# Adaptive layer norm with a Mamba block: the input of seven half sequences loaded with its channels on the partitions

## The chip, the core and the metric

The kernel runs on one core of a Trainium2 chip. The metric is the device time of one execution in microseconds (us); three executions of the kernel before gave 735.45, 736.16 and 738.33 us, so its median is 736.16 us. A profiled execution took 737.38 us, of which the profile's span covers 735.7 us.

## The reference

The input `x` has 4 sequences of 512 tokens with 512 channels. For each sequence a small matrix product of `silu(c)` with `wmod` gives six vectors over the channels: shift, scale and gate for each of two branches. The first branch is a Mamba2 mixer, the second a linear layer with binarized weights:

```
h = layernorm(x) * (1 + ca) + sa            # over the 512 channels of a token
xBCzA = h @ in_proj_w.T                     # 2048 + 1024 + 64 columns
xBC = silu(causal depthwise conv of 4 taps over the tokens)
dt = softplus(A_log); chunked scan over chunks of 128 tokens, 64 heads
x = x + ga * ((y + D * x_in) * silu(z)) @ out_proj_w.T
x = x + gb * (layernorm(x) * (1 + cb) + sb) @ (sign(w) * mean|w|).T + ...
```

The convolution and the projections want the normed input with its channels on the partitions (the contraction runs over partitions); the statistics of a token are sums over its channels. This is the place of the change.

## The kernel before

The 2048 tokens are cut into eight half sequences of T = 256 tokens (index `h`, two for each sequence, `HPB` = 2). Each half has a front (norm, projections, convolution, steps towards the scan), eight units of the scan (two chunks `c` of 128 tokens times four pairs of head groups `gp`) and a tail for each chunk (output projection, second norm, second linear layer, store).

**The order of the work.** A list of steps, one for each unit, is written out by hand at the end (L787 to L863). While the units of half `h` - 1 run as steps (h-1)*8 to (h-1)*8+7, the front of half `h` is interleaved: FRONT puts `load_x` at relative step 1, `f_norm` at 2, `f_hT` and `f_dt` at 3, then the projections `f_B`, `f_C`, `f_x`, `f_z` to step 10. For half 1 the list SECOND has `load_x` at 0, `f_norm` at 1, `f_hT` and `f_dt` at 2; half 0 has FIRST and runs ahead of all units. In one step the order written is: fronts and tails (within a step, entries of half 0 such as `load_wout` and `signs` come before those of half 1), `burst`, `stage2` of this step's unit, then `stage0` and `stage1` of the unit two steps later. The framework that builds the program lays each engine's instructions in a fixed queue; it prefers this written order, but draws an instruction ahead when its inputs and its buffer are free by its own reckoning. On the chip each queue then runs strictly in that order: an instruction that waits holds up all behind it on its engine, DMA issues on SP and POOL too.

**The lines that matter here.** `load_x` (L75) brings a half as two tiles of 128 tokens by 512 channels, tag `xa`, three buffers, on SP's queue (L79). `f_norm` (L307) calls `layer_norm` (L289): DVE's statistics (L295, L296), epsilon (L297), POOL's power of -1/2 (L298, tile `rs_a`) and DVE's in-place subtract and multiply with a value for each partition (L300). `f_hT` (L335) has TensorE turn the tiles, eight transposes of 128x128 into two PSUM tiles `phT` (L330), and ACT write `hT` from them with the modulation as scale and bias, four activations of 128x256 (L347). `hT` (tag `hT`, two buffers) holds the three last tokens of the half before in its first columns (L340, L342). `f_dt` (L353) starts with TensorE's product `pa` (L368) and goes over some twenty small DVE and ACT operations to three stores in DRAM (`sums_d`, `e_d`, `r_d`), which POOL issues for all halves but the first (L389, L393, L407). Later these come back by SP as broadcast loads: `decay` (L541, L542), `e` (L582) and `rr` (L502, tag `rr`, two buffers, read by POOL at L507). ACT makes exponentials of `decay` (L549), DVE multiplies them (L625), TensorE uses them (`py`, L212 and L215).

**Around the first halves** SP's queue also carries the late weights: `wout` (2 MB, L265, once the modulation products `pg` no longer need its place), and the four tiles `fw` of the second layer's weights (L272), which take the places of `sg` and `ab`, tiles of the gates that `late_mods` works out on DVE (L256 to L260) and stores by SP (L262).

```
for step, f, args in (FIRST, SECOND)[h] if h < 2 else FRONT:
    at(max(0, h - 1) * NU + step, f, h, *args)
...
at(2, load_wout)
for o in range(NK):
    at(o // 2 + 2, signs, o)
```

Of the kernel before, what the change touches and what calls it, by code (L numbers as in the profile page):

```python
# [11 lines left out]
F32 = mybir.dt.float32  # L12
AF = mybir.ActivationFunctionType
# [3 lines left out]
P = 128  # L17

B, L, DM = 4, 512, 512
# [3 lines left out]
KS = 4  # L23
# [3 lines left out]
T = 256  # L27
NHALF = B * L // T
HPB = L // T
NK = DM // P  # L30
# [10 lines left out]
def adaln_mamba_block(  # L41
    ctx: ExitStack,
    tc: tile.TileContext,
    x: bass.AP,
    w_inT: bass.AP,
    conv_w: bass.AP,
    conv_b: bass.AP,
# [9 lines left out]
    nc = tc.nc  # L57
# [6 lines left out]
    def bc_mid(ap, n):  # L64

        return ap.unsqueeze(1).to_broadcast([ap.shape[0], n, ap.shape[1]])

    keep = ctx.enter_context(tc.tile_pool(name="keep", bufs=1))
    dram = ctx.enter_context(tc.tile_pool(name="dram", bufs=1, space=bass.MemoryType.DRAM))
    ps = ctx.enter_context(tc.tile_pool(name="ps", bufs=5, space=PSUM))  # L70
    wk = ctx.enter_context(tc.tile_pool(name="wk", bufs=2))

    xs_of = {}

    def load_x(h, queue=nc.sync):  # L75
        tiles = []
        for j in range(2):
            xt = wk.tile([P, DM], F32, tag="xa", name=f"x_{h}_{j}", bufs=3)
            queue.dma_start(xt, x[h * T + j * CH : h * T + (j + 1) * CH, :])  # L79
            tiles.append(xt)  # L80
        xs_of[h] = tiles


    ct = keep.tile([P, NK, B], F32, name="ct")
    nc.sync.dma_start(ct, cT)
    load_x(0, nc.scalar)


# [29 lines left out]
    modT = keep.tile([P, 4, NK, B], F32, name="modT")  # L118
    gate_d = dram.tile([B, 3, DM], F32, name="gate_d")
    sums_d = dram.tile([NHALF, 2, NH, CH], F32, name="sums_d")  # L120
    e_d = dram.tile([NHALF, 2, NH, CH], F32, name="e_d")
    r_d = dram.tile([NHALF, NH, 2, CH], F32, name="r_d")

# [80 lines left out]
    def scale_small():  # L204

        for v in (cw, cb, zb):
            nc.vector.tensor_scalar(v, v, 0.5, None, ALU.mult)
# [9 lines left out]
    def first_row(t6, copy):  # L217

        pg = ps.tile([P, DM], F32, tag="mm", name=f"pg{t6}")
        for k in range(NK):  # L220
            mm(pg[32 * k : 32 * k + 32, :], sc[:, k, :], wms[t6, k], start=True, stop=True)
        row = wk.tile([P, DM], F32, tag="h2", name=f"row{t6}")
        copy(row, pg)
        return row

    def first_turn(t6, slot, row):

        pm = ps.tile([P, NK, B], F32, tag="mm", name=f"pm{t6}")
        for dt in range(NK):
            mm(pm[:, dt, :], row[:, dt * P : (dt + 1) * P], sel, start=True, stop=True)  # L230
        nc.vector.tensor_scalar(modT[:, slot], pm, 1.0 if t6 == 1 else 0.0, None, ALU.add)
# [54 lines left out]
        nc.scalar.activation(bwT[:, :, o * P : (o + 1) * P], pt, AF.Copy, scale=2.0 / DM)  # L286


    def layer_norm(tiles, name, into=None):  # L289
        n = len(tiles)  # L290
        st = wk.tile([P, n, 6], F32, tag=f"st{n}", name=f"st_{name}")
        mv = wk.tile([P, n, 2], F32, tag=f"mv{n}", name=f"mv_{name}")
        rs = wk.tile([P, n], F32, tag=f"rs{n}", name=f"rs_{name}")
        for j, t in enumerate(tiles):
            nc.vector.bn_stats(st[:, j, :], t)  # L295
            nc.vector.bn_aggr(mv[:, j, :], st[:, j, :])  # L296
        nc.vector.tensor_scalar(rs, mv[:, :, 1], EPS, None, ALU.add)  # L297
        nc.gpsimd.tensor_tensor(rs, rs, mhalf[:, :n], ALU.pow)  # L298
        for j, t in enumerate(tiles):
            nc.vector.tensor_scalar(  # L300
                into[j], t, mv[:, j, 0:1], rs[:, j : j + 1], ALU.subtract, ALU.mult
            )


    H = [dict(B={}, C={}, xt={}, xs={}, bt={}, z={}) for _ in range(NHALF)]

    def f_norm(h):  # L307
        H[h]["xn"] = xs_of.pop(h)
        layer_norm(H[h]["xn"], f"a{h}", H[h]["xn"])

    def f_first(h):

        f_norm(h)
        for xp in xpads:
            nc.gpsimd.memset(xp, 0.0)
        for et in decays:
            nc.gpsimd.memset(et[CH // 2 :, :, 0 : CH // 2], 0.0)
        rows = first_row(1, nc.vector.tensor_copy), first_row(0, nc.scalar.copy)
        turned = [turned_x(h, d2) for d2 in range(NK // 2)]
        first_turn(1, 1, rows[0])  # L320
        first_turn(0, 0, rows[1])
        f_hT(h, turned)
        scale_small()

    def turned_x(h, d2):
        pt = ps.tile([P, 2, T], F32, tag="mm", name=f"phT_{h}_{d2}")
        for q in range(2):
            dt = 2 * d2 + q
            for j in range(2):
                nc.tensor.transpose(  # L330
                    pt[:, q, j * CH : (j + 1) * CH], H[h]["xn"][j][:, dt * P : (dt + 1) * P], ident
                )
        return pt

    def f_hT(h, turned=None):  # L335
        b = h // HPB

        hT = wk.tile([P, NK, KS - 1 + T], F32, tag="hT", name=f"hT_{h}")
        if h % HPB == 0:
            nc.gpsimd.memset(hT[:, :, 0 : KS - 1], 0.0)  # L340
        else:
            nc.gpsimd.tensor_copy(hT[:, :, 0 : KS - 1], H[h - 1]["hT"][:, :, T:])  # L342
        for d2 in range(NK // 2):
            pt = turned[d2] if turned else turned_x(h, d2)
            for q in range(2):
                dt = 2 * d2 + q
                nc.scalar.activation(  # L347
                    hT[:, dt, KS - 1 :], pt[:, q, :], AF.Identity,
                    bias=modT[:, 0, dt, b : b + 1], scale=modT[:, 1, dt, b : b + 1],
                )  # L350
        H[h]["hT"] = hT

    def f_dt(h):  # L353

# [2 lines left out]

        hT = H[h]["hT"]

# [369 lines left out]
    def tail1(h, c):  # L729
        b = h // HPB  # L730
        x2 = tails[h, c]
        po = ps.tile([P, DM], F32, tag="mm", name=f"po_{h}_{c}")
        last = (h, c) == (NHALF - 1, 1)
        for g in range(NKI):
            if last and g == NKI - 2:

                with tc.issue_after(last_po.ins):
                    tail2(h, 0)
            last_po = mm(po, H[h]["z"][g // 2][:, g % 2, c * CH : (c + 1) * CH], wout[:, g, :],  # L739
                         start=(g == 0), stop=(g == NKI - 1))  # L740
        t = wk.tile([P, DM], F32, tag="t", name=f"t_{h}_{c}", bufs=1)
        nc.vector.tensor_mul(t, po, gates[b][:, 0, :])
        nc.vector.tensor_add(x2, x2, t)
        layer_norm([x2], f"f{h}_{c}", [t])
        nc.gpsimd.tensor_add(x2, x2, gates[b][:, 2, :])
        tails[h, c] = (x2, t)
        if last:
            with tc.issue_after(last_po.ins):
                tail3(h, 0)
# [31 lines left out]
    def behind(h, f, *args):  # L781
# [4 lines left out]

    FRONT = [  # L787
        (1, load_x, ()), (2, f_norm, ()), (3, f_hT, ()), (3, f_dt, ()),
        (4, f_B, (0,)), (4, f_C, (0,)), (5, f_x, (0,)), (5, f_x, (1,)),
        (6, f_B, (1,)), (6, behind, (f_turned_sums,)), (6, f_C, (1,)), (6, behind, (f_xt, 0)),  # L790
# [4 lines left out]

    FIRST = [
        (-1, f_first, ()), (-1, first_dt, ()), (-1, f_B, (0,)), (-1, f_C, (0,)), (-1, f_x, (0,)),
        (-1, f_turned_sums, ()), (-1, f_Bt, (0,)), (-1, f_x, (1,)), (-1, behind, (f_xt, 0)),
        (-1, f_z, (0,)), (-1, behind, (f_xt, 1)),
# [4 lines left out]

    SECOND = [
        (0, load_x, ()), (1, f_norm, ()), (2, f_hT, ()), (2, f_dt, ()), (2, f_B, (0,)), (3, f_C, (0,)), (3, f_x, (0,)),
        (4, f_x, (1,)), (4, behind, (f_turned_sums,)),
        (5, f_B, (1,)),
# [31 lines left out]
    h = NHALF - 1  # L840
# [65 lines left out]
```

## Time and profile before

| | |
|---|---|
| median of three executions | 736.16 us (735.45 to 738.33) |
| profiled execution, its span | 737.38 us, 735.7 us |
| granted TensorE clock, mean | 0.993 |
| TensorE (PE) busy | 700.4 us, 95% |
| VectorE (DVE) busy | 599.5 us, 81% |
| ScalarE (ACT) busy | 522.0 us, 71% |
| GpSimd (POOL) busy | 254.8 us, 35% |
| moved by DMA | 99.24 MB, 135 GB/s in the mean |
| transposes `phT` (L330), all eight halves | 64, 273 ns median each as recorded |
| activations into `hT` (L347) | 32, 564 ns median |
| norm of `x` on DVE (L300) | 16, 546 ns median |

Busy time counts an instruction from its start to its modelled end; matmuls overlap one another, so eight of them take less time than eight times one. A stretch of the span is judged by its own rows: which engine has no gaps there, and what ended the gaps of the others. A line such as "PE pa <- ACT hT" names an instruction that sat idle and the one whose end released it.

### The profile page before, as it was taken

Reading aid. Unit: us, or ns where it says so; the run is one execution under the profiler, and the core shown is the slowest. Engines: PE = TensorE matmul, PEld = TensorE weight load, DVE = VectorE, ACT = ScalarE, POOL = GpSimd, SP = SyncE. Lnnn points to the kernel's source line nnn. Section 1 sums busy time; section 2 is a strip of 40 time slices with the busy share of each in tenths; the row PEclk is TensorE's granted clock in tenths of the full one; section 3 lists DMA queues with packets and bytes.
Section 4 is the critical chain, followed back from the end, with each engine's and each line's share of the span. In section 5 each row is a group of like instructions: output and inputs, shape, how many; then the busy total and the mean of one; then the engine's idle time right before and its main releaser. Section 6 shows DMA issues by size and latency. Waiting matters only on the chain.

```text
span 735.7 us, 15007 instructions
## 1 busy us (share of the span) xinstructions
PE 700.4 (95%) x5196; PEld 500.8 (68%) x5196; DVE 599.5 (81%) x1170; ACT 522.0 (71%) x1507; POOL 254.8 (35%) x297
## 2 busy tenths in 40 slices
PE   6999979899999999999999999999999999999997
PEld 3786746666677666677677666776667866677754
DVE  3869888876998678986899768996799867996995
ACT  2467658748696697785976787865968768788941
POOL 4021323444243332343223342433414332333652
PEclk9999989999999999999999999999999999999999
DMA  8991693535555256444644256552564537457720
GB/s 279 328 291 41 204 208 85 135 98 142 127 132 144 63 155 137 102 115 102 159 116 130 53 116 168 142 137 53 140 132 114 130 86 176 116 150 151 142 69 29
DMA packets 119067, 99.24 MB, mean 135 GB/s; under 512 B 73984, under 2 KB 97152, under 8 KB 118992
## 3 DMA queue, kind: packets, MB, share of 16 engines
q1 hardware_dynamic: 117808, 96.39, 52.3%
q0 software_dynamic: 896, 1.38, 0.7%
q8 instruction: 41, 0.67, 0.4%
q10 hardware_dynamic: 288, 0.52, 0.2%
q14 instruction: 34, 0.28, 0.1%
HBM read 92.47 MB, written 5.79 MB: 134 GB/s over the span
## 4 chain that ended last, share of the span: by engine, by line
PE 65%; ACT 16%; DVE 9%; DMA 4%; issue 4%; POOL 1%; SPq 1%; ACTq 0%; DVEq 0%; POOLq 0%
PE po L739 14%; PE pp_x L434 11%; PE pp_z L434 10%; ACT decay L549 9%; PE pp_C L434 7%; PE pp_B L434 5%; PE pf L775 3%; PE py L212 2%; PE py L215 2%; DVE decay L625 2%; ACT h L759 2%; DVE u_x L454 2%; DMA fw<-in_ffn_w 2%; ACT win L549 2%; PE gy L215 2%
## 5 line engine op out<-in xcount | busy, mean ns | idle before, releaser
L549 ACT ACTIVATE decay<-decay,st 128x128 f32<-128x128 f32 x960 | 293.9, 395 | 4.2 <-DMA decay<-sums_d 3.7
L625 DVE SCALAR_TENSOR_TENSOR decay<-decay,gm 128x1024 f32<-128x1024 f32 x120 | 160.8, 1341 | 50.3 <-ACT decay L549 47.2
L434 PE MATMUL pp_x<-hT,win 128*128 128x259 f32 x512 | 120.7, 390 | 7.3 <-DVE u_C L454 7.3
L434 PE MATMUL pp_z<-hT,win 128*128 128x256 f32 x512 | 118.1, 383 | 0.0
L434 PEld LDWEIGHTS pp_x<-hT,win 128*128 128x128 f32 x512 | 96.9, 193 | 25.2 <-ACT decay L549 7.7
L739 PE MATMUL po<-wout,z 128*128 128x512 f32 x256 | 113.8, 595 | 0.0
L434 PEld LDWEIGHTS pp_z<-hT,win 128*128 128x128 f32 x512 | 94.3, 189 | 16.3 <-issue 3.5
L675 POOL TENSOR_TENSOR z<-yt,z 128x256 f32<-128x256 f32 x62 | 62.9, 1015 | 76.1 <-DVE yt L674 57.8
L454 DVE SCALAR_TENSOR_TENSOR u_x<-pp_x,cw,u_x 128x256 f32<-128x256 f32 x192 | 83.6, 474 | 1.3 <-ACT u_x L450 0.7
L739 PEld LDWEIGHTS po<-wout,z 128*128 128x128 f32 x256 | 47.5, 190 | 53.1 <-issue 52.4
L672 POOL TENSOR_TENSOR yt<-yt,xs 128x256 f32<-128x256 f32 x46 | 41.4, 899 | 106.3 <-DVE yt L671 78.6
L507 POOL TENSOR_TENSOR xs<-u_x,rr 128x512 f32<-128x512 f32 x32 | 42.7, 1334 | 79.2 <-DVE u_x L459 61.3
L516 ACT ACTIVATE uz<-pp_z,zb 128x256 f32<-128x256 f32 x64 | 27.5, 470 | 59.0 <-PE pp_z L434 59.0
L215 PE MATMUL py<-decay,xpad 128*32 128x128 f32 x1680 | 66.3, 276 | 0.0
L434 PE MATMUL pp_B<-hT,win 128*128 128x259 f32 x256 | 63.5, 396 | 2.7 <-ACT decay L549 1.9
L434 PE MATMUL pp_C<-hT,win 128*128 128x259 f32 x256 | 59.6, 384 | 1.1 <-DVE u_x L454 1.1
L775 PE MATMUL pf<-bwT,h 128*128 128x512 f32 (+1 forms) x136 | 59.0, 578 | 1.4 <-ACT h L759 1.3
L434 PEld LDWEIGHTS pp_B<-hT,win 128*128 128x128 f32 x256 | 47.4, 193 | 14.5 <-ACT decay L549 3.1
L450 ACT ACTIVATE u_x<-pp_x,cb,cw 128x256 f32<-128x256 f32 x64 | 35.3, 560 | 30.5 <-PE pp_x L434 30.4
L434 PEld LDWEIGHTS pp_C<-hT,win 128*128 128x128 f32 x256 | 47.8, 189 | 9.4 <-PE pn L424 1.4
L679 POOL TENSOR_TENSOR xd<-xpad,st 128x256 f32<-128x256 f32 x48 | 34.1, 727 | 55.8 <-PE pst L215 28.3
L212 PE MATMUL py<-decay,xpad 128*32 128x128 f32 x240 | 47.4, 279 | 3.2 <-issue 2.2
(157 smaller groups left out, 1080.9 us busy)
## 6 DMA issues: line engine op xcount, KB each, us to landing
decay<-sums_d SPq DMA_DIRECT2D x120, 256.0 KB
decay<-sums_d SPq DMA_DIRECT2D x120, 128.0 KB
rr<-r_d SPq DMA_DIRECT2D x64, 128.0 KB
e<-e_d SPq DMA_DIRECT2D x96, 64.0 KB
win<-in_w_inT SPq DMA_DIRECT2D x4, 1024.0 KB
xr<-in_x SPq DMA_DIRECT2D x16, 256.0 KB
res<-o SPq DMA_DIRECT2D x15, 256.0 KB
x<-in_x SPq DMA_DIRECT2D x14, 256.0 KB
```

Of the source, the lines that this page charges most:

```text
L212: first = products[0]()
L215: product()
L434: last = mm(pm, win[:, k, col : col + P], H[h]["hT"][:, k, lo:], start=(k == 0), stop=(k == NK - 1))
L450: nc.scalar.activation(u[:, j, :], pm[:, KS - 1 :], AF.Identity, bias=cb[:, t : t + 1], scale=cw[:, t, KS - 1 : KS])
L454: nc.vector.scalar_tensor_tensor(u[:, j, :], pm[:, k : k + T], cw[:, t, k : k + 1], u[:, j, :], ALU.mult, ALU.add)
L507: nc.gpsimd.tensor_tensor(xs, xc, rr, ALU.mult)
L549: nc.scalar.activation(ets[r][:, i, :], ets[r][:, i, :], AF.Exp, bias=H[h]["st"][:, hd : hd + 1], scale=-1.0)
L625: nc.vector.scalar_tensor_tensor(ets[r], ets[r], 1.0, bc_mid(gm[:, r, :], HPG), ALU.min, ALU.mult)
L672: ew.tensor_add(t, t, xs)
L675: ew.tensor_mul(zg, t, zg)
L739: last_po = mm(po, H[h]["z"][g // 2][:, g % 2, c * CH : (c + 1) * CH], wout[:, g, :], start=(g == 0), stop=(g == NKI - 1))
L775: mm(pf, h2[:, k, :], bwT[:, k, cols], start=(k == 0), stop=(k == NK - 1))
```

## The change

The host hands the kernel a second copy of the input, `xT`, with channels on partitions (128 partitions, 4 groups of channels, 2048 tokens). For halves 1 to 7 `load_x` also loads `hT` itself, un-normed, by one DMA of 512 KB on SP's queue, in rows of 256 tokens (1 KB). `f_norm` works out only the statistics (no L300 on the tiles); a new tile `ms` holds mean and reciprocal deviation of the tokens, and POOL stores it to a new DRAM tensor `stat_d`, 2 KB, in which the tokens lie along a row. `f_hT` then loads `stat_d` broadcast to all partitions (256 KB, SP's queue, a tile `mr` of the tag `rr`), and DVE subtracts and multiplies it over the four groups of channels in place, two operations of 128x1024; ACT applies the modulation in place from SBUF instead of from PSUM. TensorE's eight transposes are gone for these halves. Half 0 keeps the old way.

```diff
     def load_x(h, queue=nc.sync):
...
         xs_of[h] = tiles
+        if h > 0:
+            hT = wk.tile([P, NK, KS - 1 + T], F32, tag="hT", name=f"hT_{h}")
+            queue.dma_start(hT[:, :, KS - 1 :], xT[:, :, h * T : (h + 1) * T])
+            H[h]["hT"] = hT
...
+    stat_d = dram.tile([NHALF, 2, T], F32, name="stat_d")
...
+    def statistics(tiles, name, rs):
...
         nc.vector.tensor_scalar(rs, mv[:, :, 1], EPS, None, ALU.add)
         nc.gpsimd.tensor_tensor(rs, rs, mhalf[:, :n], ALU.pow)
+        return mv
...
     def f_norm(h):
+        ms = wk.tile([P, 2, 2], F32, tag="ms", name=f"ms_{h}")
+        mv = statistics(xs_of.pop(h), f"a{h}", ms[:, 1, :])
+        nc.gpsimd.tensor_copy(ms[:, 0, :], mv[:, :, 0])
+        with nc.allow_non_contiguous_dma(reason="a token's value is on its partition"):
+            nc.gpsimd.dma_start(stat_d[h].rearrange("q (j p) -> p q j", p=P), ms)
...
     def f_hT(h, turned=None):
...
+        now = hT[:, :, KS - 1 :]
+        if not turned:
+            mr = wk.tile([P, 2, T], F32, tag="rr", name=f"mr_{h}")
+            nc.sync.dma_start(mr, stat_d[h].partition_broadcast(P))
+            nc.vector.tensor_sub(now, now, bc_mid(mr[:, 0, :], NK))
+            nc.vector.tensor_mul(now, now, bc_mid(mr[:, 1, :], NK))
+        for dt in range(NK):
+            nc.scalar.activation(
+                now[:, dt, :], turned[dt // 2][:, dt % 2, :] if turned else now[:, dt, :], AF.Identity,
+                bias=modT[:, 0, dt, b : b + 1], scale=modT[:, 1, dt, b : b + 1],
+            )
```

More of the change, by code (lines that the diff above doesn't have):

```diff
@@ L44, in adaln_mamba_block @@
     x: bass.AP,
+    xT: bass.AP,
     w_inT: bass.AP,
@@ L73, in adaln_mamba_block @@
     xs_of = {}
+    H = [dict(B={}, C={}, xt={}, xs={}, bt={}, z={}) for _ in range(NHALF)]
     def load_x(h, queue=nc.sync):
@@ L286, in turned_signs @@
         nc.scalar.activation(bwT[:, :, o * P : (o + 1) * P], pt, AF.Copy, scale=2.0 / DM)
-    def layer_norm(tiles, name, into=None):
+    def statistics(tiles, name, rs):
         n = len(tiles)
@@ L292, in layer_norm @@
         mv = wk.tile([P, n, 2], F32, tag=f"mv{n}", name=f"mv_{name}")
-        rs = wk.tile([P, n], F32, tag=f"rs{n}", name=f"rs_{name}")
         for j, t in enumerate(tiles):
@@ L298, in layer_norm @@
         nc.gpsimd.tensor_tensor(rs, rs, mhalf[:, :n], ALU.pow)
+        return mv
+    def layer_norm(tiles, name, into=None):
+        n = len(tiles)
+        rs = wk.tile([P, n], F32, tag=f"rs{n}", name=f"rs_{name}")
+        mv = statistics(tiles, name, rs)
         for j, t in enumerate(tiles):
@@ L302, in layer_norm, with f_first @@
             )
-    H = [dict(B={}, C={}, xt={}, xs={}, bt={}, z={}) for _ in range(NHALF)]
     def f_norm(h):
+        ms = wk.tile([P, 2, 2], F32, tag="ms", name=f"ms_{h}")
[3 more added lines that the diff above has]
+            nc.gpsimd.dma_start(stat_d[h].rearrange("q (j p) -> p q j", p=P), ms)
+    def f_first(h):
         H[h]["xn"] = xs_of.pop(h)
         layer_norm(H[h]["xn"], f"a{h}", H[h]["xn"])
-    def f_first(h):
-        f_norm(h)
         for xp in xpads:
@@ L336, in f_hT @@
         b = h // HPB
-        hT = wk.tile([P, NK, KS - 1 + T], F32, tag="hT", name=f"hT_{h}")
+        if turned:
+            hT = H[h]["hT"] = wk.tile([P, NK, KS - 1 + T], F32, tag="hT", name=f"hT_{h}")
+        hT = H[h]["hT"]
         if h % HPB == 0:
@@ L342, in f_hT @@
             nc.gpsimd.tensor_copy(hT[:, :, 0 : KS - 1], H[h - 1]["hT"][:, :, T:])
[L343 to L351, printed above, removed]
+        now = hT[:, :, KS - 1 :]
[9 more added lines that the diff above has]
+            )
     def f_dt(h):
@@ L883 @@
         "x": np.ascontiguousarray(np.asarray(L0_attn_input_).reshape(B * L, DM)),
+        "xT": cols(np.asarray(L0_attn_input_).reshape(B * L, DM).T),
         "w_inT": np.ascontiguousarray(np.asarray(L0_attn_in_proj_w).T),
```

## The prediction

> **What bounds the kernel now.** I read the page first, then rows by stretch, then the chain of waits and the queues around the first change of halves.
>
> ```profile
> span 735.7 us, 15007 instructions
> PE 700.4 (95%) x5196; PEld 500.8 (68%) x5196; DVE 599.5 (81%) x1170; ACT 522.0 (71%) x1507; POOL 254.8 (35%) x297
> PE   6999979899999999999999999999999999999997
> ...
> PE 65%; ACT 16%; DVE 9%; DMA 4%; issue 4%; POOL 1%; SPq 1%; ACTq 0%; DVEq 0%; POOLq 0%
> ```
>
> TensorE is all but full from the sixth slice on, and holds most of the chain. The table of busy time by stretch shows how full (us, then PE, PEld, DVE, ACT, POOL; clock; DMA share; GB/s):
>
> ```profile
> 180.00:251.50 71.50, 69.72 (x498) 50.73 (x497) 64.02 (x130) 51.79 (x150) 24.33 (x28) 1.00 0.48 119
> 251.50:270.00 18.50, 17.63 (x186) 12.13 (x184) 11.99 (x17) 16.77 (x52) 8.23 (x11) 1.00 0.50 124
> 270.00:338.00 68.00, 67.13 (x461) 48.63 (x458) 59.47 (x126) 47.77 (x137) 20.99 (x27) 1.00 0.49 118
> ```
>
> A half takes 86.5 us (the norm of half 3 ends in `hT` at 266.4, half 5 at 439.7). In the short stretch where a half begins, ACT has no gap (16.77 of 18.5) and its exponentials set the pace, yet TensorE idles only 0.87 us. In the long stretch TensorE idles 0.87 of 68 and DVE is at 87%. So TensorE's own work is what a steady half costs.
>
> **Steady halves, 2 to 7: what goes.** The transposes and what waits on them, half 3, from the timeline of TensorE:
>
> ```profile
> 264.78 1.09 PE L330 MATMUL phT<-ident,x 128*128 128x128 f32 x8
> 267.02 0.44 PE L368 MATMUL pa<-hT,win 128*64 128x128 f32 x4 [0.57 <-ACT hT L347]
> ```
>
> Eight transposes take 1.09 us together: they overlap, so the page's 273 ns each must not be added up. `pa` then idles until ACT has written `hT`; between 160 and 620 us the waits list 2.7 us for this in six halves, 0.45 each. With `hT` made long before (the statistics of half 3 end at 240.3, 26 us ahead of 266.4) this goes too: at most 1.54 us a half.
>
> What comes. DVE loses two L300 (0.546 us median) and gains two operations of 128x1024 on two SBUF tensors. The trace has that size at L625: 1.225 median, 1.34 mean beside POOL. Net 2 x 1.225 - 2 x 0.546 = +1.36 us. Its old place is in the stretch where DVE is at 87%, its new one (some 5 us after the statistics, or in DVE's gaps of the next stretch, 11.99 of 18.5) is roomier, so I count 0.3 on the path; if that cover is gone it is all 1.36. ACT's four activations (564 ns) read SBUF now: 512 columns take 630 ns from SBUF (L458) and 578 from PSUM (L493), so 4 x 0.05, nothing beside ACT's gap of 6.3 us that the timeline shows before 253.2. POOL gains a copy (0.19, as L342) and a DMA issue: 0.54 is what 64 KB in 128 rows costs at L389; 512 single values lie between that and four times it, 2.2. POOL is at 35%, and 0.54 is nearest; behind it stand `xs` and `z`, which wait for DVE anyway. SP issues two more loads (0.46 us median for L79, 0.58 for L502); the load of `hT` has its buffer from the half before last and can go as early as the first tile of `x` does (188.2 for half 3), the load of `mr` goes into SP's idle 235.8 to 249.1 before the next `decay`. DMA moves 0.77 MB more a half, 6%, at a share of 0.5. PSUM gets two tiles back; I give that nothing.
>
> Sum: -1.54 + 0.3, rounded to **-1.2 us a half, -7.2 in six**. Bounds: -1.96 (all 0.87 of idle goes as well; -11.8) and +1.36 (no gain, all of DVE; +8.2). I stay near the best because TensorE has no other gaps.
>
> A rule speaks against the new store: the Trainium skill, "DMA: Bandwidth & Descriptors", Rules for kernel authors, says that a last dimension that isn't contiguous becomes one descriptor per element and should be rearranged. No store of single values is in this trace; by that rule it is 512 descriptors in place of 128 rows, and if each cost what a row's share costs, the 2.2 us above would hold and the sum would stay, as POOL has the room.
>
> **Half 1: where the change pays.** Here the steps lie close together and the DMA queue is loaded. From the chain of waits:
>
> ```profile
> 71.79 2.56 POOL rs_a L298
> ...
> 75.13 1.50 DVE x L300
> 76.64 1.00 DVE ab L260
> 77.66 0.24 SPq L262
> ...
> 82.26 0.76 SPq L272
> 83.06 13.38 DMA fw<-in_ffn_w
> ```
>
> and SP's queue:
>
> ```profile
> 77.66 0.24 SPq L262 DMA_DIRECT2D gate_d<-ab  x1
> ...
> 80.43 1.27 SPq L502 DMA_DIRECT2D rr<-r_d  x2
> 81.79 0.41 SPq L265 DMA_DIRECT2D wout<-in_w_outT  x1
> ```
>
> Before, `x` was normed at 74.4 to 76.6, turned, and `pa` ran at 77.87; half 1's `pa`, `pp_B`, `pp_C` and the first `pp_x` filled TensorE until 92.2, and then it idled 5.36 us, to 99.41, because DVE stood in line behind `fw`, which came after 2 MB of `wout` in the same queue.
>
> After: L300 leaves DVE ahead of `ab` (2.24 us, 74.37 to 76.6), so the store of the gates, `wout` and `fw` move up by 2.2: `wout` at 79.6, `fw` landed at 94.2. The statistics end at 74.34, as before; copy 0.2, issue 0.6, landing 1.8 (median of L389; up to 8.5 in a full queue) make `stat_d` ready at 77.0. By then SP has `decay` and `rr` in hand, and `wout` and two `fw` stand ahead of `mr` in the written order; SP has followed that order here almost to the letter. So I take `mr` to be issued behind them at about 81.6 and to land behind their 2.5 MB: 94.2 + 256 KB at some 250 GB/s (1.0) = 95.2. Two DVE operations, 2.45, and the first activation, 0.56: `pa` starts at 98.3 instead of 77.87. The work that TensorE had behind it by 99.41 and now has still to do: `pa` and `pp_B` 77.87 to 83.29 (5.42), `pp_C` and `pp_x` 84.95 to 92.19 (7.24), in all 12.66. It gets 99.41 - 98.3 = 1.1 back: **+11.6 us**. The transposes here lay in what becomes idle time, so they save nothing. After its idle time TensorE ran 96 to 104 at a granted clock of 0.71 and 0.50; I take that once, before and after. `hT`'s own load follows the tiles of `x` (43 to 44.6), 30 us ahead: nothing. Bounds: -1.1 (below) and +16 (`decay` loads ahead as well, or the store landing late).
>
> Half 0 is untouched, and so is the end.
>
> The Trainium skill, "GPSIMD Engine Reference", Specifications, says that GpSimd's SBUF port contends with DVE instructions that have two SBUF inputs, which the change adds. The row agrees: POOL's L298 takes 0.71 us in the steady halves and 2.55 at 71.79, beside L259 and L625. By the rule POOL would lose up to 2 x 1.2 us a half, which its 35% hides; the sum stays.
>
> **Sum:** -7.2 + 11.6 = +4.4. The profiled execution took 737.38, 1.22 above the median of 736.16; so 741.8 against the former, **740.6** in terms of the median.
>
> **The rivals.**
> 1. *`mr` gets ahead of `wout` (faster).* `stat_d` is ready at 77.0 and `wout` goes at 79.6; if SP's order has `mr` between the `decay` loads, it lands after some 4 us (`x` took 4.13 at the start), at 82.5, `pa` starts at 85.5, and 12.66 us of work end at 98.2, where TensorE stood at 99.41 before: -1.1 in half 1. Total -8.3, **727.9**. It decides at one point: is `mr` issued before `wout`. For it: 2.6 us of room. Against it: the written order and SP's row of loads without a gap from 77.7 to 83.0. Chance 0.30.
> 2. *The transposes weren't worth anything.* Where a half begins ACT is the bound, TensorE's 1.09 us lies beside it, and DVE's two long operations stand ahead of an L625. Steady halves 0: +11.6, **747.8**; with DVE's 1.36 in full, 756.0. For it: ACT 16.77 of 18.5. Against it: TensorE 95% there. Chance 0.16.
> 3. *`mr` between `wout` and `fw`.* Lands after 2 of the 2.5 MB, 0.8 of 13.38 = 10.7 us after 80.0, plus 1.0: 91.7; `pa` at 94.7, 12.66 - 4.7 = +8.0; total +0.8, **737.0**. Against it: both `fw` stand ahead in the written order; for it: they wait for the places of `sg` and `ab`. Chance 0.17.
>
> **How the numbers follow.** The forecast has 0.37. About 0.5% (3.7 us) is what a measurement of this kernel can tell from no change. Faster is rival 1, 0.30; within 0.5% rival 3, 0.17; slower the forecast and rival 2, 0.53. The range reaches from rival 1 with somewhat more in the steady halves, 726, to rival 2, 749; its tails (DVE in full, or -11.8 with rival 1) are left out. The forecast's own range, on the slower side, is 736 to 745.
>
> **What would show it.** Steady halves: the distance from half to half falls from 86.5 to about 85.3, `pa` no longer waits for `hT`; wrong if a wait of DVE or ACT takes the place. Half 1: SP's queue shows `mr` behind `wout` and `fw`, landing near 95, DVE's subtract waits for it, TensorE idles some 15 us more between 78 and 99. If `mr` stands ahead of `wout`, rival 1 holds. DVE's two operations should take 1.2 to 1.35 us each and the store of `stat_d` 2 to 4 us; a store of 8 us or more in the steady halves would make SP wait with `decay` behind it and would upset the steady sum.

## The result and the profile after

The changed kernel takes 775.87 us (median of 4 executions, 772.98 to 776.44) against 735.81 for the kernel before beside it: ratio 1.0534, 95% interval 1.0509 to 1.0559. The profiled execution took 776.44, its span 774.7. The forecast was 740.6, the range 726 to 749: slower was right, the size wrong by 35 us. From the page of the changed kernel:

```profile
span 774.7 us, 14958 instructions
PE 699.6 (90%) x5140; PEld 499.4 (64%) x5140; DVE 610.6 (79%) x1170; ACT 525.1 (68%) x1507; POOL 275.8 (36%) x311
PE   6998099689999989898999989899999979999997
...
PE 41%; DVE 18%; ACT 16%; DMA 14%; issue 5%; POOL 3%; SPq 1%; ACTq 0%; DVEq 0%; POOLq 0%
```

TensorE is busy as long as before (699.6 us against 700.4) with 56 instructions less, at a mean granted clock of 0.97 in the place of 0.993, and now with holes; its share of the chain fell from 65% to 41% and DMA's rose from 4% to 14%. The starts of `pa` in each half (timelines of TensorE) say where:

| | half 1 | 2 | 3 | 4 | 5 | 6 | 7 | from there to the end |
|---|---|---|---|---|---|---|---|---|
| before | 77.87 | 181.97 | 267.02 | 355.27 | 440.32 | 528.57 | 613.62 | 122.1 |
| after | 97.76 | 199.12 | 290.28 | 380.52 | 470.77 | 557.90 | 649.43 | 125.3 |
| later by | 19.9 | 17.2 | 23.3 | 25.3 | 30.5 | 29.3 | 35.8 | +3.2 |

So some 17 us are lost by the start of half 2, 18.7 in the five distances from there to half 7 (3.7 each, where 1.2 of gain was forecast), 3 in the end, which the prediction called untouched.

**Half 1** went much as forecast. The queue of SP:

```profile
79.97 0.42 SPq L275 DMA_DIRECT2D wout<-in_w_outT  x1
80.45 1.54 SPq L282 DMA_DIRECT2D fw<-in_ffn_w  x2
84.35 0.40 SPq L366 DMA_DIRECT2D mr<-stat_d  x1
```

and DVE and PE in their timelines (in brackets: idle time before, and what ended it):

```profile
92.73 0.69 DVE L284 TENSOR_REDUCE alpha<-fw 128x1 f32<-128x512 f32 x1 [3.18 <-DMA fw<-in_ffn_w]
...
94.59 1.22 DVE L367 TENSOR_TENSOR hT<-hT,mr 128x1024 f32<-128x1024 f32 x1
95.84 1.23 DVE L368 TENSOR_TENSOR hT<-hT,mr 128x1024 f32<-128x1024 f32 x1
```

```profile
97.76 2.17 PE L390 MATMUL pa<-hT,win 128*64 128x128 f32 x16 [22.43 <-ACT hT L370]
```

`mr` stands behind `wout` and two `fw`, DVE stands in line behind `fw` as before, and `pa` starts at 97.76 (forecast 98.3). DVE's two operations take 1.22 us each (median), as read from L625.

**The steady halves** did not. Two halves from `pa` to `pa`, before and after, in the table by stretch (us, busy time of PE, PEld, DVE, ACT, POOL; clock; DMA share; GB/s):

```profile
181.97:355.27 173.30, 169.93 (x1276) 122.73 (x1276) 144.79 (x285) 128.77 (x375) 60.27 (x73) 1.00 0.49 120
```

```profile
199.12:380.52 181.40, 171.05 (x1264) 123.11 (x1261) 149.26 (x287) 131.24 (x381) 66.60 (x76) 0.98 0.52 124
```

TensorE idles 10.4 us in the place of 3.4. What the waits of SP's queue list, of the kernel before and then of the changed one (us in total, times, longest):

```profile
SPq L502 <- DMA r_d<-dr: 3.2, 1, 3.2
```

```profile
SPq L524 <- DMA r_d<-dr: 68.3, 9, 11.0
SPq L366 <- DMA stat_d<-ms: 40.2, 6, 9.8
```

and ACT's waits for `decay`, before in the row of L549 and after in the list of waits:

```profile
L549 ACT ACTIVATE decay<-decay,st 128x128 f32<-128x128 f32 x960 | 293.9, 395 | 4.2 <-DMA decay<-sums_d 3.7
```

```profile
ACT decay L571 <- DMA decay<-sums_d: 37.1, 19, 5.9
```

The long wait for `r_d` comes from a new order of SP's queue (runs 13 and 15) and explains little of the steady loss: run 10 has 69.4 us of it and loses 0.5 us a distance. The rows of `stat_d` give its landing, the time from issue to arrival: 2 KB take longer than 64 KB of `sums_d` in 128 rows (1.8 us median here):

```profile
DMA to landing us min/median/max: 8.3/9.2/9.4
```

Two things follow in turn. Where SP reaches `mr` soon after the store, it waits in line, and the trip (store of the statistics to DRAM, load of `mr` from it) ends on DVE; the chain of waits around half 3, its short pieces left out:

```profile
256.66 8.34 DMA stat_d<-ms
...
265.05 3.88 DMA mr<-stat_d
...
268.96 1.24 DVE hT L367
...
273.18 0.61 DVE t L764
...
276.92 0.56 DVE t L316
...
277.61 0.63 PE ph L779 x4
```

Behind DVE's subtract, in DVE's queue, stands the second norm of the half before (L764, L316), and TensorE's `ph` waits for that. Where `decay` loads are issued beside the store, they crawl. Around the store issued at 342.39, one load of 128 KB, from the chain, and the table by stretch, columns as above:

```profile
344.51 11.34 DMA decay<-sums_d
```

```profile
344.00:346.00 2.00, 2.00 (x25) 1.51 (x18) 2.00 (x6) 2.00 (x8) 1.71 (x2) 1.00 2.60 38
346.00:348.00 2.00, 2.00 (x11) 1.74 (x10) 1.88 (x3) 0.58 (x2) 2.00 (x3) 1.00 0.11 10
348.00:350.00 2.00, 2.00 (x13) 1.76 (x12) 1.16 (x3) 1.35 (x3) 1.69 (x3) 1.00 0.79 20
...
354.00:356.00 2.00, 2.00 (x6) 0.95 (x5) 0.00 (x0) 0.06 (x1) 0.00 (x0) 1.00 1.05 241
```

The store lands at 351.7. With `decay` loads pending, the DMA engines move 10 to 38 GB/s in these stretches while it is under way, and 241 after it (the DMA share is of no use in stretches so short, 2.60 in the first); DVE and ACT run dry.

### The profile page after: what moved, and what is told of

Same layout as the page of the kernel before. It is cut to its first block, busy times and chain, and to the rows that moved or that the text cites. A ratio compares the mean times of both kernels' runs of the same rounds, so it can differ in the third digit from the quotient of the medians.

```text
span 774.7 us, 14958 instructions
## 1 busy us (share of the span) xinstructions
PE 699.6 (90%) x5140; PEld 499.4 (64%) x5140; DVE 610.6 (79%) x1170; ACT 525.1 (68%) x1507; POOL 275.8 (36%) x311
## 4 chain that ended last, share of the span: by engine, by line
PE 41%; DVE 18%; ACT 16%; DMA 14%; issue 5%; POOL 3%; SPq 1%; ACTq 0%; DVEq 0%; POOLq 0%
ACT decay L571 9%; PE pp_x L456 7%; DMA decay<-sums_d 6%; PE pp_z L456 6%; PE po L761 5%; PE pf L797 5%; PE pp_C L456 4%; DVE decay L647 4%; DMA stat_d<-ms 3%; PE pp_B L456 3%; PE py L225 2%; DVE u_x L476 2%; ACT win L571 2%; PE py L222 2%; DMA mr<-stat_d 2%
## 5 line engine op out<-in xcount | busy, mean ns | idle before, releaser
L647 DVE SCALAR_TENSOR_TENSOR decay<-decay,gm 128x1024 f32<-128x1024 f32 x120 | 158.0, 1318 | 54.4 <-ACT decay L571 53.5
L456 PE MATMUL pp_x<-hT,win 128*128 128x259 f32 x512 | 118.8, 385 | 5.3 <-ACT decay L571 2.8
L456 PEld LDWEIGHTS pp_x<-hT,win 128*128 128x128 f32 x512 | 94.9, 189 | 23.2 <-ACT decay L571 5.2
L697 POOL TENSOR_TENSOR z<-yt,z 128x256 f32<-128x256 f32 x62 | 58.7, 947 | 86.4 <-DVE yt L696 67.4
L694 POOL TENSOR_TENSOR yt<-yt,xs 128x256 f32<-128x256 f32 x46 | 46.4, 1009 | 112.1 <-DVE yt L693 73.8
L456 PE MATMUL pp_B<-hT,win 128*128 128x259 f32 x256 | 65.5, 404 | 5.1 <-ACT h L781 2.5
L225 PE MATMUL py<-decay,xpad 128*32 128x128 f32 x1680 | 68.3, 283 | 0.0
L529 POOL TENSOR_TENSOR xs<-u_x,rr 128x512 f32<-128x512 f32 x32 | 47.1, 1473 | 57.9 <-DVE u_x L481 42.3
L701 POOL TENSOR_TENSOR xd<-xpad,st 128x256 f32<-128x256 f32 x48 | 40.2, 854 | 58.0 <-ACT xpad L515 32.8
L222 PE MATMUL py<-decay,xpad 128*32 128x128 f32 x240 | 48.7, 286 | 1.9 <-DVE decay L647 1.0
L225 PEld LDWEIGHTS py<-decay,xpad 128*32 128x32 f32 x1680 | 49.5, 112 | 0.2
```

Source lines behind the costliest of these rows:

```text
L222: first = products[0]()
L225: product()
L456: last = mm(pm, win[:, k, col : col + P], H[h]["hT"][:, k, lo:], start=(k == 0), stop=(k == NK - 1))
L529: nc.gpsimd.tensor_tensor(xs, xc, rr, ALU.mult)
L647: nc.vector.scalar_tensor_tensor(ets[r], ets[r], 1.0, bc_mid(gm[:, r, :], HPG), ALU.min, ALU.mult)
L694: ew.tensor_add(t, t, xs)
```

## The experiments

Three theories. **Theory 1:** the store of 512 single values costs the steady halves, by its length, by SP's wait with `decay` loads behind, and by what it does to loads beside it. **Theory 2:** DVE's longer operations, the added traffic and the new order of the queues cost them. **Theory 3:** half 1's trip is a price of its own. "Ratio" is to the kernel before, with its 95% interval; "distance" is the mean of the five from half 2's `pa` to half 7's (before 86.33 us, after 90.06).

**1. Rows in DRAM.**

```diff
-    stat_d = dram.tile([NHALF, 2, T], F32, name="stat_d")
+    stat_d = dram.tile([NHALF, P, 2, 2], F32, name="stat_d")
...
-            nc.gpsimd.dma_start(stat_d[h].rearrange("q (j p) -> p q j", p=P), ms)
+        nc.gpsimd.dma_start(stat_d[h], ms)
...
+            by = mr.rearrange("a q t -> a (q t)").rearrange("a (p q j) -> a q j p", q=2, j=2)
...
```

> The statistics lie in DRAM as 128 rows of 16 bytes, one for each partition, in the place of 512 single values of 4 bytes; the broadcast load is flat, and VectorE reads it by steps. All else is as in the changed kernel. Theory 1 (the store of single values takes 8.3 to 9.4 us, SyncE waits for it in line, and loads issued beside it crawl): the store lands in 2 to 4 us, SyncE's waits for stat_d fall from 40.2 us to under 15, ScalarE's waits for the decay loads from 37.1 to under 10, and of the 22 us that halves 2 to 7 lost some 20 come back, with 5 to 7 more in half 1: 748 to 756 us. Theory 2 (VectorE's longer operations in place, the order of the queue and the 768 KB more for each half cost the time, not the form of the store): 768 us or more.

Measured: 753.9 us, ratio 1.0236 (1.0217 to 1.0256); distance 86.63. The landing:

```profile
DMA to landing us min/median/max: 2.1/2.9/3.8
```

SP's waits for `stat_d` fell to 12.0 us, ACT's for `decay` to 14.7 (under 10 was expected). 22 us hang on the store's form: theory 1 for the steady halves.

**2. Half 1 turned on TensorE as before.**

```diff
-        if h > 0:
+        if not (h < 2):
             hT = wk.tile([P, NK, KS - 1 + T], F32, tag="hT", name=f"hT_{h}")
...
     def f_norm(h):
+        if h < 2:
+            H[h]["xn"] = xs_of.pop(h)
+            layer_norm(H[h]["xn"], f"a{h}", H[h]["xn"])
+            return
...
```

> Half 1 is turned on TensorE as before (as is half 0); the store of single values stays for halves 2 to 7. Theory 3 (half 1's way through DRAM, queued between the last weights, costs the 17 us that its pa starts late beyond half 0's): 757 to 761 us, with half 1's pa at 78 to 80 us and the later halves losing 22 us as now. If half 1's delay only pulled forward a loss that the halves after it would have had in any case: 768 us or more.

Measured: 770.69, ratio 1.0471 (1.0445 to 1.0497). `pa` of half 1 is back at 76.71, but half 2's starts 114.5 us later (after: 101.4): only 5 of 17 us come back. With the slow store in place the next half loses what half 1 gained.

**3. Both.** 

> Both edits: rows of 16 bytes, and half 1 turned on TensorE. Theory 1 with theory 3: nothing but the steady halves of the prediction is left, 736 - 7 = 729 us, within 728 to 738. Theory 2 (the longer operations in place cost the steady halves their 22 us): 752 us or more.

Measured: 740.2, ratio 1.0061 (1.0046 to 1.0076). Without the slow store, half 1 was worth 13.7 us (753.9 to 740.2). But 740 isn't 729: the distance is 86.41, not 85.1, and the end is 125.3. DVE reads `mr` with steps of 16 bytes here and takes 2.05 us (median) for each operation in the place of 1.22.

**4. The kernel before with the store alone.** In the kernel before, `f_norm` also makes `ms` (two copies on GpSimd) and stores it as the changed kernel does:

```diff
+            ms = wk.tile([P, 2, 2], F32, tag="ms", name=f"ms_{h}")
+            nc.gpsimd.tensor_copy(ms[:, 0, :], mv[:, :, 0])
+            nc.gpsimd.tensor_copy(ms[:, 1, :], rs)
...
+                nc.gpsimd.dma_start(stat_d[h].rearrange("q (j p) -> p q j", p=P), ms)
```

> The kernel before, with nothing of the change but the store of 512 single values for halves 1 to 7, which no instruction reads (and the two small copies on GpSimd ahead of it). Theory 1: the store takes 8 to 9 us here too, nothing waits for it, but the decay loads that fall beside it land in up to 11 us instead of 2; 739 to 750 us. Theory 2: within 1.5 us of the kernel before.

Measured: 744.63, ratio 1.0121 (1.0100 to 1.0142); the store lands in 8.5 us here too. But 7.3 us of it are lost between half 1 and half 2, and the distance is 86.49: from half 3 on no `decay` load is issued while the store is under way, and there it costs at most 0.16 us. In halves 1 and 2 loads fall beside it (stores issued at 74.32 and 162.27). In half 2 an issue on SP that otherwise takes 0.6 us takes 3.32 (SP's timeline), and a load issued next 6.86 (the chain):

```profile
166.10 3.32 SPq L550 DMA_DIRECT2D decay<-sums_d  x1
```

```profile
170.14 6.86 DMA decay<-sums_d
```

**5. Tokens in pairs.** The tiles of `x` hold tokens 2p and 2p+1 on partition p, and the store is 256 pieces of 8 bytes (half 1 the old way).

```diff
+            rows = rows[j * CH : (j + 1) * CH, :] if h < 2 else rows.rearrange("(p j) d -> p j d", j=2)[:, j, :]
...
-            nc.gpsimd.dma_start(stat_d[h].rearrange("q (j p) -> p q j", p=P), ms)
+            nc.gpsimd.dma_start(stat_d[h].rearrange("q (p j) -> p q j", p=P), ms)
```

> As the kernel with rows and the old way for half 1, but the tiles of x for the statistics hold tokens 2p and 2p+1 on partition p, so that the store is 256 pieces of 8 bytes into the two rows of the changed kernel, the broadcast load is as in the changed kernel, and VectorE reads without steps. If the landing goes by the number of pieces (2.3 us for 128, 8.6 for 512), it is 4 to 5 us here; VectorE's two operations are back at 1.2 to 1.3 us each (2.05 with steps). If these 1.6 us a half were on the path: 732 to 737 us; if what is left after the store is mended comes from somewhere else (the new order of the queues), 738 to 743.

Measured: 745.87, ratio 1.0132 (1.0091 to 1.0172); landing 4.1 us. So the landing grows with the pieces: 2.3 for 128 (run 3), 4.1 for 256, 8.6 for 512 (run 2). The 745.87 lie above both expectations, slower than run 3 in the same order of SP's and GpSimd's queues, though DVE's operations are short again. That doesn't show that those 1.6 us a half are off the path, for the longer landing costs too: DVE waits 11.9 us for `mr` here, 4.3 in run 3.

**6. `mr` of half 1 ahead of `wout`.** As 1, with its load written right behind the store in `f_norm`.

> As the kernel with rows, but half 1's load of mr is written right behind the store of its statistics, so that it stands ahead of wout and the fw tiles in SyncE's queue. Theory 3 in the prediction's words (half 1 pays because mr lands behind 2.5 MB): pa of half 1 starts at 81 to 86 us instead of 93.95, and the time falls by 10 to 13, to 741 to 744 us. If the delay comes from the round trip itself and not from its place in the queue: 750 us or more.

Measured: 753.83, ratio 1.0244 (1.0216 to 1.0271): the start of `pa` came as theory 3 says (85.72 in the place of 93.95), the gain didn't. Half 2 came 107.7 us later, not 100.5. Between them DVE waits for half 2's own `mr`, and TensorE's `ph` behind it (the waits of DVE, then of PE, between 84 and 193 us):

```profile
DVE hT L377 <- DMA mr<-stat_d: 6.5, 1, 6.5
```

```profile
PE ph L790 <- DVE t L316: 8.1, 2, 6.7
```

Run 1 has neither wait.

**7. `mr` issued by GpSimd.** `nc.sync.dma_start(mr, ...)` becomes `nc.gpsimd.dma_start(mr, ...)` in the changed kernel.

> The changed kernel with its store of 512 single values, but all loads of mr are issued by GpSimd, so that GpSimd, which is busy 36% of the time, waits for the store in the place of SyncE. If the line at SyncE (decay loads behind the waiting mr) is what costs the steady halves, most of their 22 us come back, half to half at 86 to 88 us: 750 to 762 us. If the store hurts by itself, by holding the DMA engines while other loads run: 768 us or more.

Measured: 806.92, ratio 1.0952 (1.0911 to 1.0994), far above the first line. The wait didn't go, it changed engines: GpSimd waits 36.8 us for the store, `mr` comes later, and DVE, with all its work behind, waits for it:

```profile
DVE hT L367 <- DMA mr<-stat_d: 75.4, 7, 13.6
```

So the second line's number (768 or more) came, but not for its reason, and the run doesn't tell line from store; 10 and 11 do.

**8. Without the trip.** The changed kernel less the copy, the store, the load of `mr` and L367, L368.

> The changed kernel without the copy, the store, the load of mr and VectorE's two operations: hT is modulated without having been normed, so subtracting the mean and multiplying by the reciprocal deviation are left out for halves 1 to 7. It is what is left when the transposes are gone and nothing stands in their place. The prediction's gain (1.54 us a half, seven times): 725 to 729 us; with 3 us at the end, as the other kernels of this family show there because the builder lays the queues in another order, up to 731. Rival 2 of the prediction (the transposes were worth nothing): 734 us or more.

Measured: 735.63, ratio 0.9993 (0.9977 to 1.0009). With nothing in the transposes' place there is no gain. `pa` of half 1 is 4.2 us earlier and half 2 another 2.9, but the distance is 86.65 and the end 126.3.

**9. Transposes that nobody reads.** As 8, with `turned_x(h, d2)` called in `f_hT` for halves 1 to 7.

> The kernel without the trip through DRAM, and with the eight transposes of halves 1 to 7 put back on TensorE, whose output nobody reads (hT is modulated without having been normed, as there). Prediction's steady step (TensorE's 1.09 us a half are on the path): slower than without them by seven times 1.09, 742 to 744 us. If TensorE's time is not what a half costs here (the gain is given back in waits elsewhere): within 2 us of 735.6.

Measured: 738.25, ratio 1.0022 (1.0000 to 1.0044), between the two expectations, because three things move: the distance grows from 86.65 to 87.83, by 1.18, near the 1.09 of the timeline; half 2's `pa` comes 1.5 us earlier; the end shrinks from 126.3 to 122.3. No instruction was added in the end. So something else moves the time as well: SP's and GpSimd's queues have another order than in 8. TensorE's busy time accounts for 0.84 of the 1.18 and its idle time for 0.34, and that the sum is so near 1.09 can be chance.

**10 and 11. A ready `mr`, without and with the store.** `mr` is loaded from a row of weights; 10 also leaves out the copy and the store. All that is left stands in the order of the changed kernel on every queue.

```diff
-            nc.sync.dma_start(mr, stat_d[h].partition_broadcast(P))
+            nc.sync.dma_start(mr, w_inT[h, 0 : 2 * T].rearrange("(q t) -> q t", q=2).partition_broadcast(P))
```

> The changed kernel, instruction by instruction and in the same order on every queue, but mr is loaded from a row of the weights, which is ready at any time, and the copy and store of the statistics are left out. So mean and reciprocal deviation are replaced by weights, and nothing waits for a trip. It shows what VectorE's two operations, the loads and the order of the queues cost, without the store and without the wait. Theory 1 (store and wait are what costs): 735.6 us without the operations, plus 1 to 2 us a half, 738 to 748. Theory 2 (the operations and the order cost it): 760 or more.

> As the kernel with the ready mr, plus the copy and the store of 512 single values, which nobody reads (mr still comes from a row of weights). Same instructions and same order as the changed kernel; only the wait of mr for the store is missing. If the store hurts by itself, by slowing the loads beside it: 10 us or more above the kernel with the ready mr, 755 to 770. If the wait (SyncE in line with decay loads behind, and the length of the trip in half 1) is what costs: within 5 us of that kernel, and the changed kernel's 775.9 stand 25 us or more above.

Measured: 755.81, ratio 1.0247 (1.0214 to 1.0281), and 766.92, ratio 1.0405 (1.0375 to 1.0434). 10 lies between its two lines; 11 meets its first (11.1 above 10). Together they split the loss (times are medians; the last column is from the profiled executions):

| step | us | by | where it lies |
|---|---|---|---|
| before | 735.8 | | |
| no trip (8) | 735.6 | -0.2 | half 1 gains, order and end give it back |
| + ready `mr`, L367, L368 (10) | 755.8 | +20.2 | `pa` of half 1: 73.71 to 93.76; distance 86.65 to 86.81 |
| + the store, unread (11) | 766.9 | +11.1 | `pa` of half 1 +4.0, of half 2 another +2.1, 0.6 a distance |
| + the wait for it (after) | 775.9 | +9.0 | 2.6 a distance; half 2 gains 2.0 |

With DVE's two operations and the ready load a distance is 0.16 us longer than in 8, and 0.48 longer than in the kernel before, where the change loses 3.73: theory 2 explains little of the loss. The store costs 20.1, about half with nobody waiting for it (the trace shows loads crawl beside it) and half by the wait. Part of the wait's 2.6 a distance is clock: from half 2's `pa` to half 7's the same TensorE instructions are busy for 425.3 us at a mean clock of 0.98 after, 419.3 at 1.00 in 11, which makes 1.2 a distance. Half 1 costs 20 above the kernel without a trip even if `mr` is ready.

**12. Half 1's statistics a step earlier.** As 6, and `f_norm` of half 1 stands at step 0 of SECOND.

> A candidate: rows of 16 bytes, all of halves 1 to 7 in the changed way, and half 1's statistics written one step earlier with the load of mr right behind, so that its trip lies before the place where hT is wanted. If half 1's cost is the length of its trip behind the statistics: pa of half 1 at 74 to 76 us as in the kernel without the trip (73.71), 731 to 736 us. If half 1 is held by something else: 740 or more.

Measured: 747.96, ratio 1.0166 (1.0118 to 1.0214). `pa` of half 1 at 79.08, not 74 to 76; half 2 came 107.1 later, as in 6, and DVE waits 6.3 us for half 2's `mr` here too.

**13 to 15. Order, and place.** In 13 (as 8) and 15 (as 3) the first load of `rr` in each half is held behind `decay` loads that stood ahead of it before; 14 is 10 with half 1's load of `mr` written in `f_norm`, ahead of `wout`.

```diff
+            with tc.issue_after(sums_in[h - 1, 1, 2]) if h and j == 0 else nullcontext():
                 nc.sync.dma_start(rr[:, r, :], ...)
```

> The kernel without the trip (hT modulated without having been normed), with half by half the first load of rr held behind the decay loads that stood ahead of it in the kernel before; the builder laid it ahead of them when the transposes were gone. If this order (SyncE waits up to 10 us for the store of r_d with decay loads behind) takes the transposes' gain: half to half 85.5 us instead of 87, 727 to 731 us. If not: within 2.5 us of 735.6.

> The kernel with a ready mr (a row of weights in the place of the statistics), in which half 1's load of mr stands ahead of wout and fw in SyncE's queue. If the place behind 2.5 MB is half 1's price, the 20 us above the kernel without the trip go: pa of half 1 at 73 to 78 us, 735 to 742 us. If not: 750 or more.

> A candidate: rows of 16 bytes, halves 0 and 1 turned on TensorE, and the first load of rr of each half held behind the decay loads as in the kernel before. If the order takes the gain: 731 to 736 us against 740.2 without the hold. If not: 738 to 742.

Measured: 13: 725.42, ratio 0.9852 (0.9825 to 0.9879), just below its line and 10 us faster than 8 by one order: distance 85.58, end 122.6. SP's waits for the store of `r_d` in 8 and in 13:

```profile
SPq L516 <- DMA r_d<-dr: 44.4, 5, 10.5
```

```profile
SPq L517 <- DMA r_d<-dr: 4.3, 1, 4.3
```

With the transposes gone, `rr` stands ahead of two pairs of `decay` loads, and SP waits up to 10.5 us with these behind it. The new order costs 8 its 10.2 us; how, isn't shown. The wait alone can't be it: at the first such place (184 to 194 us in 8, 10.3 us for `r_d`) SP stands still as long in 13, 8.0 us for TensorE and 2.5 for DVE to free a place for `decay`, and in 15 the same wait goes with almost no gain. (The hold shifts the other queues a little as well.)

14: 745.03, ratio 1.0109 (1.0068 to 1.0151), between its two lines: `pa` of half 1 from 93.76 to 81.92, and 10.8 of the 20.2 us come back, and stay. The place behind 2.5 MB is a good half of half 1's price. The rest lies on the way from `mr`, issued at 72.39, over DVE's operations (78.76) and ACT (81.27); in 8, without a trip, ACT has written `hT` by 67.5.

15: 738.97, ratio 1.0043 (1.0023 to 1.0063), in its second line. SP's wait for `r_d` falls from 67.0 us in 3 to 3.2, the distance only from 86.41 to 86.33. The end is 122.9 in the place of 125.3, but `pa` of halves 1 and 2 came 1.7 and 3.0 us later than in 3: a gain of 1.2 us between the medians, if any. No version that does the whole norm beat the kernel before.

## Why the prediction was wrong, step by step

- **What bounds the kernel:** right. From half 2's `pa` to half 7's TensorE is busy 423.6 us before and 417.8 in 13, where nothing stands in the transposes' place: 1.17 less a distance, for 1.09 of transposes. Its idle time there is 8.0 and 10.1 us, 0.42 a distance more. (A half by the two times named is 86.65 us, not 86.5; nothing rests on it.)
- **Half 1:** right in place, and so close in time (`pa` 97.76 against 98.3) in part by luck. `mr` stood behind `wout` and `fw`, but DVE never waits for it: its own line behind `fw` sets the time, and 4.0 of the 97.76 come from the store's effect on the loads (93.76 in 10, 97.76 in 11), which the sum hadn't. The price of 11.6 was too low: with `mr` ready and the same order half 2's `pa` is 13.1 late, with the store 17.2. The 12.66 us of work leave out what else stands in TensorE's line behind `pa`, the `gy`, `py` and `pst` that ran before at 83.29 to 84.95 and 92.19 to 94.05, 3.5 us together, and now from 105.70 on.
- **Rival 1** (`mr` ahead of `wout` gains 1.1, by its own numbers 1.2): its start came (85.5; 6 gave 85.72, with a faster store and longer DVE operations than it reckoned with), its end didn't: the 8 us were lost again by half 2, whose own trip held DVE.
- **DVE's net +1.36, counted as 0.3:** right in size; 1.22 us an operation, and with a ready `mr` 0.16 a distance (10 against 8, whose queues have another order).
- **The store: the step that failed.** I bounded its issue on POOL from both sides (0.54 to 2.2; it took 0.84) and gave its landing the 1.8 us of L389, a store of 64 KB in 128 rows. The landing is 9.2, and the steady sum gave the way through DRAM no price at all: `mr` was to go into SP's idle time. I had set aside what the Trainium skill, "DMA: Bandwidth & Descriptors", Rules for kernel authors, says against a last dimension that isn't contiguous, by the share of an issue, as if POOL alone paid. The landings agree with the rule (2.3, 4.1 and 8.6 us for 128, 256 and 512 pieces); the number of descriptors stands in no view. I even named the sign ("a store of 8 us or more") and left it out of the range, though nothing in the trace excluded it. It costs 20.1 of the 35 us that the forecast was off; most of the rest is the steady gain that didn't come and the end.
- **The gain of 1.54 a half:** half of it, and only in another order. I kept all queues as they were and struck out instructions; the builder lays them anew, and in 8 a distance is 0.32 longer than before. With `rr` held (13) it is 85.58, 0.75 shorter: TensorE's work went, but the 0.45 that `pa` waits for `hT` didn't turn into time. That 13 gains 11 us, as seven times 1.54 would, is luck: most of it lies ahead of half 2, whose `pa` comes 9.5 us earlier. Rival 2 had the number (nothing gained) by another mechanism, ACT as the bound; ACT's busy time is the same in 13 (321.9 us from half 2's `pa` to half 7's, 321.1 before), which speaks against it.
- **"So is the end":** wrong by 3.2 us. It goes with the order: 13 and 15, which hold `rr`, and 9 end at 122.3 to 122.9, all others of this family at 125.2 to 126.7, whether or not they have a trip.

Open: how half 2 in 6, 12 and 15 loses what half 1 gains, beyond DVE's wait for `mr`; how the place of `rr` costs 8 its 10 us, and why 15 gains so little by the same hold. No run takes the trip's wait out of DVE's queue while keeping the norm.

## What to carry to other kernels

Count the pieces of a store, not its bytes, and price its landing from a row with as many pieces; if there is none, the upper end belongs in the range, together with what is loaded beside it and who stands in line for it. A trip through DRAM ahead of an in-order engine is paid by whatever stands behind the first instruction that needs it; moving the wait to another queue (7) changed who paid, and cost 31 us more. Where a builder orders the queues by its own reckoning, taking instructions out is also a change of order: compare the order of every queue before crediting a gain.

## What the runs showed that was not expected

- 2 KB stored in 128 pieces of 16 bytes land in 2.2 to 3.4 us, in 256 of 8 bytes in 4.1, in 512 of 4 bytes in 8.5 to 10.0 (medians of the runs).
- While the 512 pieces are under way, all DMA runs at 10 to 38 GB/s around 344 to 350 us (241 just after), a load of 128 KB takes up to 11.46 us (at 131.08 in the chain), and an issue on SP 3.32 in the place of 0.6.
- DVE's 128x1024 operation takes 2.05 us in the median if one operand is read in steps of 16 bytes, 1.22 if not.
- After TensorE's idle time in half 1 of the changed kernel (75.3 to 97.8 us) its work began at half clock: the mean granted clock is 0.69 from 78 to 84, 0.50 from 84 to 102, 0.81 from 102 to 108.
